# A three-layer block on one core: second evictions given to ScalarE and GpSimd, attention's weights prepared among the experts, more row buffers

## The chip, the cores and the metric

The kernel runs on one core of a Trainium2 chip. The metric is the device time of one execution in microseconds, lower is better. The core has TensorE (PE; its weight loads are listed as PEld), VectorE (DVE), ScalarE (ACT), GpSimd (POOL) and SyncE (SP), each with an instruction queue of its own that it works through in order, and DMA queues that move data between device memory and the on-chip memory SBUF. Matmul results land in PSUM.

## The reference: what is computed

```python
x = x + 0.5 * ffn(layernorm(x), router_w, rg, ru, rd, sg, su, sd)
x = x + attn(layernorm(x), w_qkv, ln_w, w_proj)
x = x + 0.5 * ffn(layernorm(x), router_w, rg, ru, rd, sg, su, sd)
```

`x` is (2, 2048, 256), that is 4096 tokens of width 256. `ffn` is a mixture of experts: a router takes the best two of 8 experts for each token, each expert takes at most 640 tokens in their order, computes `silu(x @ rg) * (x @ ru) @ rd` with inner width 1024, and its result is scaled by the routing weight and added to the token's row. A shared expert of inner width 2048 runs over all tokens and is added. `attn` works in groups of 64 tokens with 16 heads of width 16: one product for q, k and v, a root-mean-square norm of q and k with the weight `ln_w`, causal softmax inside the group, and an output product with `w_proj`.

## The kernel before, in words

Every float32 operand of a large product is split into two float16 parts (`split`, line 102 on ScalarE and 103 on VectorE), and three of the four partial products are summed in PSUM. The work runs in four phases.

- Phase a (0 to about 300 us): 32 row tiles of 128 tokens are loaded, normalised, routed, and their rows (tile `X`: 256 values and four tags) are scattered by GpSimd (line 283) to the experts' lists in device memory. Beside this, the shared expert runs over the first 4 of 8 blocks of 512 tokens.
- Phase b (to 614 us): the eight experts of the first feed-forward layer. Each runs 8 chunks of 128 inner columns. A chunk loads `re` and `re2` (lines 396 and 399), splits them into `wc` and `wd`, runs the gate and up products (`gate_up`, line 302), and one chunk later the down product (`down`, line 326). After the last chunk, five row tiles leave PSUM: VectorE or ScalarE writes a scaled row tile `eo` (lines 421 and 419), and GpSimd adds it to the rows of the accumulator `acc` by an indirect DMA (line 422). `eo` has 4 buffers.
- Phase c (to 1461 us): the shared expert over the last 4 blocks of the first layer and the first 7 of the second, 11 blocks in all. Between its chunks stand the steps of 32 attention tiles (`attn_tile`), each of which also normalises and routes its rows for the second layer and writes them to `X` (6 buffers). `attn_init` prepares attention's weights at the start: six pieces of float32 weights are loaded (`rq` line 442, `rp` line 448) and split.
- Phase d (to the end): the eight experts of the second layer, and the last block of the shared expert with `late=10`, which loads the residual rows in its tenth chunk.

A shared block has 16 chunks. In each, the first product `pgu` passes through ScalarE and VectorE (`sl`, lines 309, 310, 315; in phase a lines 313 and 315), ScalarE rounds it to `hh` (line 317) and VectorE takes the remainder `hl` (line 318). The down product of a chunk is emitted after the gate and up products of the following one (`defer`). After the last down product, both output tiles `outs[0]` and `outs[1]` are evicted: VectorE adds the scaled PSUM tile to the residual tile `xr` (line 359), and SP stores it (line 362).

The order of instructions on each engine comes from a planner that simulates the program while it is compiled: the written order gives the priority, and an instruction that the planner holds to be ready may go ahead of one that is not. The engines then follow that order. `drive` sets how the steps of attention tiles are woven into the chunks (one round of steps for every three chunk steps in phase c). A pool gives each named tile a number of buffers, and a new tile waits until the oldest buffer's users are done. Indirect adds to `acc` are put in a group of accesses that need not wait for one another.

Of the kernel before, what the change touches and what calls it, by code (L numbers as in the profile page):

```python
# [8 lines left out]
F32 = mybir.dt.float32  # L9
F32R = mybir.dt.float32r  # L10
F16 = mybir.dt.float16
# [4 lines left out]
ALU = mybir.AluOpType  # L16
# [4 lines left out]
P = 128  # L21
H = 256
# [3 lines left out]
WS = 16.0  # L26
XP = UP * WS
NB = 8
BT = 512
# [8 lines left out]
class Net:  # L38
# [306 lines left out]
    def shared(self, b, xb, src, dst, tanh=False, late=2):  # L345
        nc = self.nc
        outs = [self.ps_out.tile([P, BT], F32, name="po", tag="po") for _ in range(2)]
        for c in range(16):
            if c == late:
                res = self.res_load(src, b)  # L350
            h = [a[:, 0:BT] for a in self.hbuf()]
            yield from self.gate_up(self.sgu[:, c], xb, h, tanh)

            def fin(c=c, h=h):
                self.down(outs, 4, h, self.sdw[:, :, c], c, 16)
                if c < 15:
                    return
                for i in range(2):
                    nc.vector.scalar_tensor_tensor(
                        out=res[i], in0=outs[i].rearrange("p (t f) -> p t f", f=H), scalar=0.5 / WS,  # L360
                        in1=res[i], op0=ALU.mult, op1=ALU.add)
                    nc.sync.dma_start(
                        out=dst[b * BT + i * 2 * P:b * BT + (i + 1) * 2 * P].rearrange("(t p) f -> p t f", p=P),
                        in_=res[i])

            self.defer(fin)
            yield
# [14 lines left out]
            out=w, in0=tag[:, :, 3], scalar=float(e), in1=tag[:, :, 1], op0=ALU.is_equal, op1=ALU.mult)  # L382
        nc.vector.tensor_tensor(out=w, in0=w, in1=tag[:, :, 2], op=ALU.add)

    def experts(self, R, rg, ru, rd, cur):

        nc = self.nc
        for e in range(E):
            x, ids, wts = cur["x"], cur["id"], cur["w"]
            outs = [self.ps_out.tile([P, BT], F32, name="po", tag="po") for _ in range(3)]  # L390
            cur = {}
            nxt = self.expert_load(R, e + 1, cur) if e < E - 1 else iter(())
            for c in range(8):
                r = self.raw.tile([P, 2, 2, P], F32, name="re", tag="raw")
                for i, s in enumerate((rg, ru)):
                    nc.sync.dma_start(
                        out=r[:, i], in_=s[e, :, c * P:(c + 1) * P].rearrange("(k p) f -> p k f", p=P))
                r2 = self.raw.tile([P, H], F32, name="re2", tag="raw2")
                nc.sync.dma_start(out=r2, in_=rd[e, c * P:(c + 1) * P])
                wc = self.raw.tile([P, 2, 2, 2, P], F16, name="wc")  # L400
                self.split(wc[:, 0], wc[:, 1], r)
                wd = self.raw.tile([P, 2, H], F16, name="wd")
                self.split(wd[:, 0], wd[:, 1], r2)
                h = self.hbuf()
                for t0, n in SUBS:
                    hs = [a[:, t0:t0 + n] for a in h]
                    for _ in self.gate_up(wc, x[:, :, t0:t0 + n], hs):
                        pass

                def fin(e=e, c=c, h=h, wd=wd, outs=outs, ids=ids, wts=wts):  # L410
                    self.down(outs, 5, h, wd, c, 8)
                    if c < 7:
                        return
                    key = R["key"], e
                    for t in range(5):
                        eo = self.raw.tile([P, H], F32, name="eo", bufs=4)
                        o = outs[t // 2][:, (t % 2) * H:(t % 2 + 1) * H]
                        if t % 2:
                            nc.scalar.activation(eo, o, AF.Copy, scale=wts[:, t:t + 1])
                        else:  # L420
                            nc.vector.tensor_scalar_mul(eo, o, wts[:, t:t + 1])
                        i = nc.gpsimd.indirect_dma_start(  # L422
                            out=R["acc"][:, :], out_offset=bass.IndirectOffsetOnAxis(ap=ids[:, t:t + 1], axis=0),
                            in_=eo, in_offset=None, bounds_check=T - 1, oob_is_err=False, compute_op=ALU.add).ins
                        if t:
                            self.tc.declare_no_dep(i, group=str(key), reason="an expert's tokens are distinct")
                        self.tc.add_to_no_dep_group(str(key), i)

                self.defer(fin)
                next(nxt, None)  # L430
            for _ in nxt:
                pass

    def attn_init(self, w_qkv, ln_w, w_proj):
        nc = self.nc
        a = self.at
        self.wqkv = a.tile([P, 2, 2, 3 * H], F16, name="wqkv")
        self.wpr = a.tile([P, 2, 2, H], F16, name="wpr")
        for k in range(2):
            for c0, n in ((0, 2 * H), (2 * H, H)):  # L440
                r = a.tile([P, 2 * H], F32, name="rq", tag="q32")[:, :n]
                nc.sync.dma_start(out=r, in_=w_qkv[k * P:(k + 1) * P, c0:c0 + n])
                self.split(self.wqkv[:, 0, k, c0:c0 + n], self.wqkv[:, 1, k, c0:c0 + n], r)
        wp = w_proj.rearrange("(j r c) f -> r j c f", r=2, c=16)
        for k in range(2):
            r = a.tile([P, H], F32, name="rp", tag="yy")
            for j in range(8):
                nc.sync.dma_start(out=r[j * 16:(j + 1) * 16], in_=wp[k, j])
            self.split(self.wpr[:, 0, k], self.wpr[:, 1, k], r)
        self.lnw = a.tile([P, H], F32, name="lnw")  # L450
        nc.sync.dma_start(out=self.lnw, in_=ln_w.unsqueeze(0).to_broadcast([P, H]))
        self.mask = a.tile([P, 64], F32, name="mask")
        m2 = self.sm.tile([P, 64], F32, name="m2", bufs=1)
        for m, base in ((self.mask, 0), (m2, -64)):
            nc.gpsimd.memset(m, 0.0)
            nc.gpsimd.affine_select(
                out=m, in_=m, pattern=[[-1, 64]], compare_op=ALU.is_ge, fill=-3.0e38,
                base=base, channel_multiplier=1)
        nc.vector.tensor_copy(self.mask[64:P], m2[64:P])
        self.QK = a.tile([P, 24, P], F16, name="QK")  # L460
        nc.gpsimd.memset(self.QK, 0.0)
        self.V2 = []
        for i in range(2):
            v = a.tile([P, 2, 2, 8, 34], F16, name=f"V2{i}")
            nc.gpsimd.memset(v[:, :, 0, :, 32:33], 1.0)
            nc.gpsimd.memset(v[:, :, 1, :, 32:33], 0.0)
            self.V2.append(v)
# [199 lines left out]
def run_slots(tiles, until):  # L667
    while not until():
        for _ in tiles.steps():
            pass  # L670


def drive(main, tiles, rate):

    credit = 0.0
    side = iter(())
    for _ in main:
        credit += 1.0
        for _ in range(2):
            if next(side, "end") == "end":  # L680
                break
        if credit >= rate:
            for _ in side:
                pass
            credit -= rate
            if not tiles.done():
                side = tiles.steps()
    for _ in side:
        pass
# [3 lines left out]
def macaron(ctx, tc, x, w_qkv, ln_w, w_proj, router_w, rg, ru, rd, sg, su, sd, out):  # L693
    nc = tc.nc
    x = x.rearrange("b s h -> (b s) h")
    out = out.rearrange("b s h -> (b s) h")
    n = Net(ctx, tc)
    R1 = n.route_init(0)
# [32 lines left out]
    def ready(h, b):  # L731
        return lambda: (h, b) in fbs and fbs[(h, b)]["n"] == 4

    def all_shared(key, b, src, dst, **k):
        yield from n.shared(b, fbs[key]["xb"], src, dst, **k)
        used.add(key)
# [10 lines left out]
    with n.phase("a", BT, 2, 10):  # L747
# [16 lines left out]
        cur = {}  # L764
        for _ in n.expert_load(R1, 0, cur):
            pass
    with n.phase("b", CAP, 3):
        n.experts(R1, rg, ru, rd, cur)
    with n.phase("c", BT, 2, 6, SLC):
        n.attn_init(w_qkv, ln_w, w_proj)  # L770
        tiles = Tiles(tile2, 32, GAP_C)
        for b in range(NA, NB):
            drive(all_shared((1, b), b, R1["acc"], R1["acc"], tanh=True), tiles, RATE_C)
        for b in range(NC):
            run_slots(tiles, ready(2, b))
            drive(all_shared((2, b), b, x2, R2["acc"], tanh=True), tiles, RATE_C)
        run_slots(tiles, tiles.done)
        cur = {}
        for _ in n.expert_load(R2, 0, cur):
            pass  # L780
# [16 lines left out]
SLC = 2  # L797
# [28 lines left out]
```

## Time and profile before

| What | Value |
|---|---|
| Median of 3 runs | 1846.73 us (1844.07 to 1847.13) |
| The profiled execution's own time | 1844.18 us |
| Its span from first to last instruction | 1842.5 us |
| TensorE busy | 1782.8 us (97%) |
| VectorE busy | 1204.9 us (65%) |
| ScalarE busy | 952.2 us (52%) |
| GpSimd busy | 769.5 us (42%) |
| Granted TensorE clock | 0.999 |
| Scatters of rows (line 283) | 128, 1026 ns each on GpSimd |
| Adds to the accumulators (line 422) | 80, about 1610 ns each on GpSimd |

The page lists busy times of each engine, and groups of instructions by line. A row of the timeline gives start, duration, engine, line, operation, output and inputs, and in brackets the time the engine stood idle before it and what ended that wait. Matmuls overlap, so a busy TensorE in the page can still have short gaps between the starts of its matmuls.

### The profile page before, as it was taken

To read this page: it belongs to the slowest core of one execution; us is meant where nothing else is said; L and a number is where in the kernel's file an instruction comes from. 1 tells how busy PE (TensorE), PEld (TensorE's weight loads), DVE (VectorE), ACT (ScalarE), POOL (GpSimd) and SP (SyncE) were. 2 spreads that over 40 slices of the span, in tenths; PEclk is the share of its full clock that TensorE was granted. 3 is DMA by queue.
4 is the path that set the end of the run, shared out by engine and by line. 5 is a ranking of instruction groups with operands and counts; after the bars stand their busy time and mean duration, and the time that the engine had idled before them with its cause. 6 is when DMAs were issued, how large, how long until landed. Compare 5 with 4: busy or idle time off the path is not lost.

```text
span 1842.5 us, 37619 instructions
## 1 busy us (share of the span) xinstructions
PE 1782.8 (97%) x13722; PEld 1197.0 (65%) x13722; DVE 1204.9 (65%) x2869; ACT 952.2 (52%) x2055; POOL 769.5 (42%) x1104
## 2 busy tenths in 40 slices
PE   6989999999999899999999999999999999999999
PEld 3545656777777556666666666666665677777765
DVE  7665545666666567787877878787755565666643
ACT  5333324555555365766666666666333455555542
POOL 7776540111221244567667676776530011112210
PEclk9999999999999999999999999999999999999999
DMA  9753022445554246767585776757213044455420
GB/s 291 224 142 94 12 63 69 107 107 114 128 115 101 58 80 110 118 114 158 104 148 117 140 137 119 152 98 125 48 30 87 27 111 111 108 112 127 104 47 12
DMA packets 447514, 196.61 MB, mean 107 GB/s; under 512 B 302369, under 2 KB 444381, under 8 KB 447264
## 3 DMA queue, kind: packets, MB, share of 16 engines
q1 hardware_dynamic: 429664, 173.03, 42.7%
q0 software_dynamic: 17664, 21.17, 6.7%
q8 instruction: 107, 1.75, 0.4%
q14 instruction: 79, 0.65, 0.1%
HBM read 81.04 MB, written 52.85 MB: 73 GB/s over the span
## 4 chain that ended last, share of the span: by engine, by line
PE 57%; POOL 12%; issue 11%; DVE 10%; DMA 5%; ACT 4%; SPq 1%; POOLq 0%; DVEq 0%; another core or an unknown queue 0%; ACTq 0%
PE pgu L302 36%; PE po L326 18%; POOL xg L283 3%; DVE sl L315 2%; DVE sl L310 1%; POOL X L281 1%; DVE hl L318 1%; POOL rstd L142 1%; POOL S L546 1%; DMA y<-in_L_attn_x_dram 1%; ACT hh L317 1%; PE pqk L599 1%; ACT sl L309 1%; POOL e L557 1%; DMA xg<-X,di 1%
## 5 line engine op out<-in xcount | busy, mean ns | idle before, releaser
L302 PE MATMUL pgu<-xb,sgu 128*128 128x512 f16 x3072 | 743.5, 380 | 20.3 <-DVE sl L310 8.0
L317 ACT CAST hh<-sl 128x512 f16<-128x512 f32 (+2 forms) x512 | 272.9, 533 | 485.4 <-DVE sl L315 471.4
L302 PE MATMUL pgu<-xe,wc 128*128 128x384 f16 (+1 forms) x3072 | 497.0, 299 | 0.8
L302 PEld LDWEIGHTS <-sgu 128*128 128x128 f16 x3072 | 294.0, 98 | 295.7 <-issue 29.6
L315 DVE SCALAR_TENSOR_TENSOR sl<-pgu,sl 128x512 f32<-128x512 f32 (+2 forms) x512 | 300.6, 587 | 215.5 <-PE pgu L302 180.1
L318 DVE TENSOR_TENSOR hl<-sl,hh 128x512 f16<-128x512 f32 (+2 forms) x512 | 311.0, 608 | 160.1 <-ACT hh L317 153.3
L326 PEld LDWEIGHTS <-hh 128*128 128x128 f16 x3328 | 319.8, 98 | 114.9 <-ACT hh L317 13.9
L302 PEld LDWEIGHTS <-wc 128*128 128x128 f16 x3072 | 300.5, 98 | 94.1 <-issue 1.9
L326 PE MATMUL po<-sdw,hh 128*128 128x256 f16 x2048 | 349.9, 273 | 10.1 <-ACT hh L317 6.8
L326 PE MATMUL po<-sdw,hl 128*128 128x256 f16 x1024 | 247.5, 273 | 11.7 <-DVE hl L318 10.4
L326 PE MATMUL po<-wd,hh 128*128 128x256 f16 x1280 | 223.6, 273 | 0.0
L326 PEld LDWEIGHTS <-hl 128*128 128x128 f16 x1664 | 162.8, 98 | 57.2 <-DVE hl L318 23.3
L422 POOL DMA_INDIRECT out_dram<-eo,eid x40 | 64.1, 1604 | 314.3 <-DVE hl L318 244.9
L313 ACT ACTIVATE sl<-pgu 128x384 f32<-128x384 f32 (+1 forms) x336 | 158.9, 473 | 56.7 <-PE pgu L302 27.6
L422 POOL DMA_INDIRECT acc<-eo,eid x40 | 64.8, 1621 | 266.2 <-DVE hl L318 227.4
L283 POOL DMA_INDIRECT xg<-X,di x128 | 131.3, 1026 | 66.2 <-issue 27.5
L326 PE MATMUL po<-wd,hl 128*128 128x256 f16 x640 | 152.5, 273 | 2.1 <-DVE hl L318 1.9
L310 DVE SCALAR_TENSOR_TENSOR sl<-sl,pgu 128x512 f32<-128x512 f32 x176 | 120.0, 682 | 45.4 <-ACT sl L309 43.2
L309 ACT ACTIVATE sl<-pgu 128x512 f32<-128x512 f32 x176 | 104.3, 593 | 42.3 <-PE pgu L302 36.3
L102 ACT ACTIVATE wc<-re 128x512 f16<-128x512 f32 x128 | 80.5, 629 | 78.0 <-PE pgu L302 51.2
L103 DVE SCALAR_TENSOR_TENSOR wc<-re,wc 128x512 f16<-128x512 f32 x128 | 88.3, 690 | 25.9 <-ACT wc L102 25.7
L546 POOL TENSOR_TENSOR S<-S,amx 128x1024 f32<-128x1024 f32 x32 | 62.1, 1939 | 79.1 <-DVE amx L545 72.1
(141 smaller groups left out, 1740.6 us busy)
## 6 DMA issues: line engine op xcount, KB each, us to landing
re<-in_L_ffn_rg_dram SPq DMA_DIRECT2D x128, 128.0 KB
re<-in_L_ffn_ru_dram SPq DMA_DIRECT2D x128, 128.0 KB
re<-in_L_ffn_rd_dram SPq DMA_DIRECT2D x128, 128.0 KB
xg<-zero SPq DMA_DIRECT2D x16, 650.0 KB
y<-acc SPq DMA_DIRECT2D x64, 128.0 KB
y<-in_L_attn_x_dram SPq DMA_DIRECT2D x32, 128.0 KB
acc<-xr SPq DMA_DIRECT2D x16, 256.0 KB
out_dram<-xr SPq DMA_DIRECT2D x16, 256.0 KB
```

The lines of the kernel that those rows point to most:

```text
L103: nc.vector.scalar_tensor_tensor(out=lo, in0=src, scalar=WS, in1=hi, op0=ALU.mult, op1=ALU.subtract)
L283: i = nc.gpsimd.indirect_dma_start(out=R["xg"][:, :], out_offset=bass.IndirectOffsetOnAxis(ap=di[:, t, k:k + 1], axis=0), in_=X, in_offset ...
L302: nc.tensor.matmul(p, lhsT=wc[:, w, i, k, :], rhs=x[:, 2 * a + k, :], start=(j == 0), stop=(j == 5))
L309: nc.scalar.activation(s, p, AF.Tanh, scale=0.5 / XP)
L310: nc.vector.scalar_tensor_tensor(out=s, in0=s, scalar=1.0, in1=p, op0=ALU.add, op1=ALU.mult)
L313: nc.scalar.activation(s, p, AF.Silu, scale=1.0 / XP)
L315: nc.vector.scalar_tensor_tensor(out=s, in0=ps[1], scalar=1.0 / XP / (2.0 * XP if tanh else 1.0), in1=s, op0=ALU.mult, op1=ALU.mult)
L317: nc.scalar.copy(h[0], s)
L318: nc.vector.tensor_tensor(out=h[1], in0=s, in1=h[0], op=ALU.subtract)
L326: nc.tensor.matmul(o, lhsT=h[a][:, t * P:(t + 1) * P], rhs=wd[:, w], start=(c == 0 and j == 0 and t % 2 == 0), stop=(c == nch - 1 and j == 2),
L422: i = nc.gpsimd.indirect_dma_start(out=R["acc"][:, :], out_offset=bass.IndirectOffsetOnAxis(ap=ids[:, t:t + 1], axis=0), in_=eo, in_offset ...
L546: self.anchor = nc.gpsimd.tensor_tensor(out=S, in0=S, in1=mx.unsqueeze(2).to_broadcast([P, 16, 64]), op=ALU.subtract)
```

## The change

Four edits. The second of the two evictions of a shared block is done by ScalarE, which scales the PSUM tile into a new SBUF tile `ev`, and GpSimd, which adds it to the residual tile; the last block of the kernel (`late=10`) keeps VectorE for both. The loads and splits of attention's weights move from `attn_init` into a generator `attn_weights`, of which `experts` takes one step in the sixth chunk of each expert of phase b, six steps in all; the raw pieces use the buffers of the experts' raw weights (`raw` and `raw2`, two each), and the split weights stay in the pool that lives for the whole kernel. `eo` gets 5 buffers instead of 4, and the fifth indirect add of an expert is no longer exempt from waiting for the four before it. `X` gets 10 buffers in phase c instead of 6.

```diff
                 for i in range(2):
-                    nc.vector.scalar_tensor_tensor(
-                        out=res[i], in0=outs[i].rearrange("p (t f) -> p t f", f=H), scalar=0.5 / WS,
-                        in1=res[i], op0=ALU.mult, op1=ALU.add)
+                    o = outs[i].rearrange("p (t f) -> p t f", f=H)
+                    if i == 0 or late > 2:
+                        nc.vector.scalar_tensor_tensor(
+                            out=res[i], in0=o, scalar=0.5 / WS, in1=res[i], op0=ALU.mult, op1=ALU.add)
+                    else:
+                        ev = self.tok.tile([P, 2, H], F32, name="ev", bufs=1)
+                        nc.scalar.mul(ev, o, 0.5 / WS)
+                        nc.gpsimd.tensor_tensor(out=res[i], in0=ev, in1=res[i], op=ALU.add)
                     nc.sync.dma_start(
...
-    def experts(self, R, rg, ru, rd, cur):
+    def experts(self, R, rg, ru, rd, cur, also=iter(())):
...
-                        eo = self.raw.tile([P, H], F32, name="eo", bufs=4)
+                        eo = self.raw.tile([P, H], F32, name="eo", bufs=5)
...
-                        if t:
+                        if 0 < t < 4:
                             self.tc.declare_no_dep(i, group=str(key), reason="an expert's tokens are distinct")
                         self.tc.add_to_no_dep_group(str(key), i)
 
                 self.defer(fin)
                 next(nxt, None)
+                if c == 5:
+                    next(also, None)
...
-    def attn_init(self, w_qkv, ln_w, w_proj):
-        nc = self.nc
-        a = self.at
-        self.wqkv = a.tile([P, 2, 2, 3 * H], F16, name="wqkv")
-        self.wpr = a.tile([P, 2, 2, H], F16, name="wpr")
+    def attn_weights(self, w_qkv, w_proj):
+
+        nc = self.nc
+        self.wqkv = self.cst.tile([P, 2, 2, 3 * H], F16, name="wqkv")
+        self.wpr = self.cst.tile([P, 2, 2, H], F16, name="wpr")
         for k in range(2):
             for c0, n in ((0, 2 * H), (2 * H, H)):
-                r = a.tile([P, 2 * H], F32, name="rq", tag="q32")[:, :n]
+                r = self.raw.tile([P, 2 * H], F32, name="rq", tag="raw")[:, :n]
                 nc.sync.dma_start(out=r, in_=w_qkv[k * P:(k + 1) * P, c0:c0 + n])
                 self.split(self.wqkv[:, 0, k, c0:c0 + n], self.wqkv[:, 1, k, c0:c0 + n], r)
+                yield
         wp = w_proj.rearrange("(j r c) f -> r j c f", r=2, c=16)
         for k in range(2):
-            r = a.tile([P, H], F32, name="rp", tag="yy")
+            r = self.raw.tile([P, H], F32, name="rp", tag="raw2")
             for j in range(8):
                 nc.sync.dma_start(out=r[j * 16:(j + 1) * 16], in_=wp[k, j])
             self.split(self.wpr[:, 0, k], self.wpr[:, 1, k], r)
+            yield
+
+    def attn_init(self, ln_w):
+        nc = self.nc
+        a = self.at
...
-        n.experts(R1, rg, ru, rd, cur)
-    with n.phase("c", BT, 2, 6, SLC):
-        n.attn_init(w_qkv, ln_w, w_proj)
+        n.experts(R1, rg, ru, rd, cur, n.attn_weights(w_qkv, w_proj))
+    with n.phase("c", BT, 2, 10, SLC):
+        n.attn_init(ln_w)
```

## The prediction

> **What bounds the kernel now.** I read the page's engine totals, then busy time by stage. The stages start at 300 (first experts), 614 (attention beside shared blocks), 1345 (attention done), 1461 (second experts) and 1781 us (last shared block).
>
> ```profile
> PE 1782.8 (97%) x13722; PEld 1197.0 (65%) x13722; DVE 1204.9 (65%) x2869; ACT 952.2 (52%) x2055; POOL 769.5 (42%) x1104
> ...
> 0.00:300.00 300.00, 268.51 (x1774) 157.50 (x1775) 174.79 (x540) 107.25 (x228) 172.47 (x363) 0.99 0.47 131
> 300.00:614.00 314.00, 312.89 (x2486) 242.78 (x2485) 191.08 (x413) 166.36 (x393) 58.73 (x41) 1.00 0.47 105
> 614.00:650.00 36.00, 30.14 (x173) 16.19 (x171) 20.39 (x46) 12.42 (x25) 13.75 (x16) 1.00 0.41 92
> 650.00:1345.00 695.00, 682.54 (x5715) 431.70 (x5714) 538.34 (x1309) 442.67 (x921) 445.18 (x608) 1.00 0.64 118
> ```
>
> Columns: window, length, then PE, PEld, DVE, ACT, POOL busy. TensorE is the bound everywhere; only its idle time can be won. Since recorded matmuls overlap, I take gaps from matmul starts: back to back, 512 columns are 0.216 us apart and 256 columns 0.109. Summing what exceeds that gives 36.4 us idle before 300, 2.1 in the first experts, 7.2 in 614 to 650, 15.3 in 650 to 1345, 3.0 to 1461, 2.6 in the second experts. Next, who makes the gaps: the waits of 300 to 614, 1461 to 1842 and 614 to 650.
>
> ```profile
> DVE eo L421 <- DMA acc<-eo,eid: 13.4, 7, 2.6
> ...
> DVE eo L421 <- DMA out_dram<-eo,eid: 17.9, 8, 3.8
> ...
> ACT wqkv L102 <- DMA rq<-in_L_attn_w_qkv_dram: 10.3, 4, 4.0
> ```
>
> The fifth scaled row waits for the first scatter to free one of four buffers (total us, times, longest); ScalarE waits for attention's raw weights. The timeline shows what TensorE pays, at 347, 623 and 637, then at a block boundary of the attention stage.
>
> ```profile
> 346.89 0.48 DVE L421 TENSOR_SCALAR eo<-po,ew 128x256 f32<-128x256 f32 x1 [2.60 <-DMA acc<-eo,eid]
> 347.76 0.28 PE L326 MATMUL po<-wd,hl 128*128 128x256 f16 x1 [0.54 <-DVE hl L318]
> ...
> 622.55 0.48 DVE L421 TENSOR_SCALAR eo<-po,ew 128x256 f32<-128x256 f32 x1 [2.33 <-DMA acc<-eo,eid]
> 623.69 2.75 PE L302 MATMUL pgu<-xb,sgu 128*128 128x512 f16 x12 [1.96 <-DVE sl L315]
> ...
> 637.81 0.61 PE L326 MATMUL po<-sdw,hh 128*128 128x256 f16 x4 [1.16 <-ACT hh L317]
> ...
> 1018.73 0.68 DVE L540 TENSOR_TENSOR S<-psc,mask 128x512 f32<-128x512 f32 x1
> 1019.32 0.68 DVE L359 SCALAR_TENSOR_TENSOR xr<-po,xr 128x512 f32<-128x512 f32 x1
> 1019.92 0.68 DVE L318 TENSOR_TENSOR hl<-sl,hh 128x512 f16<-128x512 f32 x1
> 1020.66 0.28 PE L326 MATMUL po<-sdw,hl 128*128 128x256 f16 x1 [0.71 <-DVE hl L318]
> ```
>
> A block's second eviction stands on VectorE just ahead of the hl that TensorE waits for.
>
> [...] the accumulating scatter here frees its row after 3.9 us (618.65 to 622.55), so I use 3.9.
>
> **The change part by part**, against the profiled execution, 1844.18 us (span 1842.5 and 1.7 around it).
>
> Five scaled rows: the 15 waits above vanish, and so should the gaps behind them: 0.71+0.30, 0.24+0.30 and 0.25+0.30 in the first experts, 0.69+0.30, 1.03+0.30 and 0.30 in the second: 4.7 us. The other waits (mostly 1.6 us) cost TensorE nothing. I take -4.3 (bounds -3.0 and -4.7). The stall goes to GpSimd: t=4 is no longer exempt, so its scatter waits until t=0 to 3 have landed. Queued behind it are the next experts' id casts, not needed for some 30 us. At the end of the first experts scatter 3 starts at 624.21, lands at 628.1, and scatter 4 lands at 632.0 instead of 629.97. In the last block, scatters land some 4 us later than 1790 and the residual load (issued at 1790) is used at 1838: 44 us of cover; without it, 4 us.
>
> Start of the attention stage: gaps of 0.55+2.12 come from the fifth row; 0.57, 1.33, 0.86, 0.22, 1.02, 0.50 (4.5) fall while ScalarE and VectorE take the weights between shared chunks. The first attention load, now behind 4 rq and 16 rp issues on SP (635.51), can go at 632.0. GpSimd's constant fills shift behind scatter 4, to about 634; first used at 655.8. What is late next is the first rows' load and VectorE's statistics behind it (1.4 us waited for y now). I take 2.5 of the 2.7 and 2.7 of the 4.5: -5.2 (bounds -2.7 and -7.2).
>
> Weights among the first experts: ScalarE gets 2x0.629+2x0.416+2x0.414 = 2.9 us, VectorE 2x0.693+2x0.411+2x0.554 = 3.3, SP 4x0.346+16x0.414 = 8.0, in a 314 us stage where they are busy 166 and 191 us and SP issues three loads per 4.9 us chunk. Each piece takes one of two raw buffers, so the next chunk's load starts a chunk later; it took two chunks ahead, so one is left. The danger is ScalarE standing in order before a piece that has not landed: at 633 to 642 it waited 4.0, 2.45 and 3.64. From the fifth-row waits TensorE forgives some 1.6 (2.13 cost 0.54). So 0 to 6x2.4 = 14; I take +1.2, because these loads go out a chunk ahead.
>
> Evictions, 15 of 16 blocks: VectorE loses 0.68 per block; ScalarE gains an estimated 0.60 (128x512 f32 from PSUM, L309: 593 ns), GpSimd 1.18 (128x512 QK subtract, L524). At six boundaries (858 to 1262) hl costs TensorE 0.87; without L359 hl can start 0.6 sooner: 6x0.6 = 3.6. ScalarE idles 1.04 us there before hh (1018.25), GpSimd 3.3 before S (1021.88), so both fit. The second store, and SP behind it, waits for GpSimd instead of VectorE: about 1019.3 against 1020.0. But VectorE's gap may be filled by the 1.21 us maximum (L545) instead, and ScalarE's slot may be missed. I take -2.6 (bounds -6 and, as below, +20).
>
> In the first stage the same edit adds 4x1.18 to GpSimd (busy 172 of 300), among scatters whose landing ScalarE's X waits for (42.6 us there), and takes 2.7 from VectorE: between -2.7 and +4.7, I take +1.0.
>
> Ten X rows: in 650 to 1345 no X write waits for a scatter, so 0; the transfers are already covered by a tile interval of some 20 us. Uncovered, it would be the first stage's wait, up to 6.2 us each.
>
> Sum: -4.3-5.2+1.2-2.6+1.0 = -9.9, so 1834.3 profiled. The median of the runs stands 1.00138 above the profiled execution (1846.73/1844.18): **1836.8**.
>
> **Rivals.** (A) As summed, chance 0.58, 1831 to 1842. (B) More: with VectorE lighter and attention started earlier, the 1.04 us gaps ahead of each boundary (L310 late behind ScalarE) close too, 10 of the 15.3 us instead of 2.6: 1844.18-17.3 = 1826.9, 1829.4 as median. For it: both gaps recur every 80.7 us. Against: the first comes from ScalarE, which gets more work. 0.15. (C) A wait takes the place of the one removed: each of the six weight pieces holds ScalarE 3.1 us, 1.5 beyond what is forgiven, +9 for +1.2: -2.1, median 1844.6, within noise. For it: the 10.3 us now. Against: one chunk of lead. 0.14. (D) Slower: ScalarE's eviction, in order, lands ahead of the gate's L309 and hh at each boundary of the attention stage (+0.60), and VectorE's gap takes L545 (+1.21): 1.8 us for 11 blocks, +20 in place of -2.6: 1856.9, median 1859. It decides from (7.3+3.7)/11 = 1.0 us per block. For it: ScalarE already makes L309 late at 1016.11. Against: the idle 1.04 us. 0.13.
>
> **How the numbers follow.** 0.2% (3.7 us) is about what a measurement here can tell from no change. A and B are faster, 0.73; C is no change, 0.14; D slower, 0.13. 1829 to 1849 holds A, most of B and C, and the near end of D.
>
> **What would show it.** Right: no eo wait ended by a scatter's landing on VectorE, such waits on GpSimd's fifth scatter instead; no wqkv wait after 614 and under 3 us idle in 614 to 650; hl gaps at boundaries under 0.4; first y load near 632. Wrong: ScalarE waits for rq or rp among the experts with gaps behind them; gaps above 1.9 us per boundary; GpSimd's add ending the waits of SP's transposes; more than 40 us idle before 300.

## The result and the profile after

The changed kernel takes 1852.99 us (median of 6 runs, 1850.99 to 1856.16), beside 1846.25 us for the kernel before on the same chip. The ratio is 1.0037, with a 95% interval of 1.0023 to 1.0050: a little slower, where the prediction had 1836.8. The profiled executions stand at 1844.18 us before and 1856.16 us after (spans 1842.5 and 1854.4), so the two traces have 12 us between them. That is more than the 6.7 us between the medians, since the profiled execution of the changed kernel is the slowest of its six. A few lines have moved in the new code: the fifth-row eviction is now line 426 (VectorE) and 424 (ScalarE), the indirect add 427, the id cast 385, the tag load 380, the raw attention weights `rq` 449 and `rp` 456, the first eviction of a block 361, and the new pair 365 and 366.

The engine totals of the changed kernel, then the stages that the prediction showed, with the same columns (window, length, PE, PEld, DVE, ACT, POOL busy, PEclk, DMA share, GB/s). The windows follow the stages; that of the first experts is longer by 13 us:

```profile
PE 1788.9 (96%) x13722; PEld 1200.8 (65%) x13722; DVE 1203.8 (65%) x2854; ACT 961.9 (52%) x2070; POOL 793.5 (43%) x1119
```

```profile
300.00:627.00 327.00, 317.83 (x2492) 245.35 (x2491) 195.12 (x419) 169.96 (x401) 57.06 (x42) 0.98 0.46 104
627.00:663.00 36.00, 31.32 (x174) 17.60 (x172) 18.52 (x45) 12.53 (x24) 16.75 (x20) 0.91 0.38 81
663.00:1345.00 682.00, 672.77 (x5649) 425.75 (x5647) 526.34 (x1277) 439.67 (x915) 454.09 (x602) 1.00 0.60 117
```

Same matmuls, same count, but TensorE is 9.2 us short of its stage among the first experts (1.1 before), and the granted clock, 1.00 in both stages before, is 0.98 there and 0.91 at the start of attention. Two things are mixed in that: TensorE waits, and after some waits its matmuls run slower.

The table gives, for each stage, its length and the time by which the starts of matmuls exceed back-to-back spacing (idle and slow together), worked out in the manner of the prediction (its figures for the kernel before are up to 1.8 us lower). Starts are taken because the records overlap: in the kernel before a matmul of 512 columns in line 302 is recorded with 380 ns on average, and back to back the starts lie 216 ns apart. First experts means from the first to the last gate and up matmul of the phase.

| Stage | before: length, lost | after: length, lost | lost, change |
|---|---|---|---|
| up to the first experts | 297.5, 38.2 | 298.6, 39.2 | +1.0 |
| first experts | 316.2, 2.2 | 328.6, 14.7 | +12.5 |
| next 36 us (attention starts) | 36, 7.3 | 36, 8.1 | +0.8 |
| rest, to the second experts | 806.4, 19.1 | 803.6, 15.6 | -3.5 |
| second experts | 316.9, 2.9 | 318.4, 4.4 | +1.5 |
| last block, to the last matmul | 65.3, 0.6 | 65.3, 0.6 | 0 |

**The first experts hold nearly the whole loss;** what the other stages gain and lose comes to about nothing. The fifth-row waits on VectorE are gone, as predicted. The waits of 302 to 627 us name what came instead (us in total, times, longest):

```profile
ACT wqkv L102 <- DMA rq<-in_L_attn_w_qkv_dram: 20.4, 4, 6.3
...
POOL acc L427 <- DMA acc<-eo,eid: 7.0, 2, 3.6
```

ScalarE stands before the split of attention's raw weights for 20.4 us, twice the 10.3 us that it stood there at the start of attention before. The waits of SP's own queue in the same window tell why the weights are late:

```profile
SPq L380 <- POOL eid L385: 27.3, 4, 7.4
```

SP stands before the load of an expert's tags, because the tag's buffer is held by GpSimd's id cast. This wait is not new. In the kernel before it is nearly as long:

```profile
SPq L375 <- POOL eid L380: 26.7, 4, 7.1
```

What is new is that a load of raw weights now stands behind three of these four tag loads, and that the first of them goes out 4.3 us later, counted from the start of the experts. The timeline around 360 us puts the links in order (start, duration, engine, line; in brackets the idle time before it and what ended it):

```profile
355.08 1.55 POOL L427 DMA_INDIRECT acc<-eo,eid  x1 [3.54 <-DVE sl L315]
359.14 0.19 POOL L385 CAST eid<-tag 128x5 int32<-128x5 f32 x1 [2.51 <-DMA acc<-eo,eid]
359.36 0.37 SPq L380 DMA_DIRECT2D tag<-xg  x1
359.84 0.46 SPq L449 DMA_DIRECT2D rq<-in_L_attn_w_qkv_dram  x1
362.50 0.42 ACT L102 ACTIVATE wqkv<-rq 128x256 f16<-128x256 f32 x1 [6.14 <-DMA rq<-in_L_attn_w_qkv_dram]
363.37 1.03 PE L326 MATMUL po<-wd,hh 128*128 128x256 f16 x4 [2.70 <-ACT hh L317]
364.20 2.12 PE L302 MATMUL pgu<-xe,wc 128*128 128x384 f16 x6
...
368.67 1.14 PE L302 MATMUL pgu<-xe,wc 128*128 128x384 f16 x6
```

Read it from the top. The fifth indirect add, no longer exempt, stands 3.54 us until its predecessors have landed and starts at 355.08. (The bracket names VectorE's `sl`; but in e1 below, where this add is exempt, it starts 0.30 us after its predecessor's end.) Its landing frees the id buffer that the next expert's cast at 359.14 needs; in the kernel before, whose experts begin 1.0 us earlier, that cast stood at 353.83. The cast frees `tag`; SP issues the tag load, and behind it, in order, the `rq` load. ScalarE reaches the split of `rq` 6.14 us before the data, and the `hh` that TensorE needs is queued behind it. TensorE loses 2.87 us at 360.34, 3.19 at 403.76 and 2.54 at 447.82, in three of the eight experts. The first of the four pieces, at 319 us, was waited for 2.15 us and cost nothing.

The last two lines of the fence show a second loss. The same six matmuls of 384 columns take 2.12 us just after the gap and 1.14 us four microseconds later: their starts lie at double spacing. This lasts some 3 us after each of the three gaps and loses 1.4, 1.7 and 1.7 us; the last section shows when it happens. A fourth gap, of 1.23 us at 303.67, belongs to the evictions (below).

**At the start of attention** the weight gaps have gone, but a wait of VectorE has grown from 1.4 to 7.5 us. Timeline of the changed kernel:

```profile
642.00 1.55 POOL L427 DMA_INDIRECT acc<-eo,eid  x1 [2.89 <-issue]
645.80 0.33 SPq L487 DMA_DIRECT2D y<-acc  x1
647.86 0.43 DVE L137 BATCH_NORM_STATS2 st<-y 128x6 f32<-128x256 f32 x1 [7.51 <-DMA y<-acc]
648.92 2.19 PE L302 MATMUL pgu<-xb,sgu 128*128 128x512 f16 x6 [3.45 <-DVE sl L310]
```

The first row load follows the landing of the fifth indirect add, and VectorE stands in order before the statistics of those rows while the shared block's `sl` waits behind them. TensorE loses 3.61 and 1.27 us, and 2.6 more at double spacing.

**Inside the attention stage** the evictions do what was forecast. One block boundary, from the timeline:

```profile
1030.90 0.68 DVE L361 SCALAR_TENSOR_TENSOR xr<-po,xr 128x512 f32<-128x512 f32 x1
1031.02 0.62 ACT L317 CAST hh<-sl 128x512 f16<-128x512 f32 x1 [1.04 <-DVE sl L315]
...
1031.50 0.68 DVE L553 TENSOR_TENSOR S<-psc,mask 128x512 f32<-128x512 f32 x1
...
1031.55 0.59 ACT L365 ACTIVATE ev<-po 128x512 f32<-128x512 f32 x1
1032.04 0.59 ACT L309 ACTIVATE sl<-pgu 128x512 f32<-128x512 f32 x1
1032.10 0.68 DVE L318 TENSOR_TENSOR hl<-sl,hh 128x512 f16<-128x512 f32 x1
1032.22 1.69 POOL L366 TENSOR_TENSOR xr<-ev,xr 128x512 f32<-128x512 f32 x1 [0.86 <-ACT ev L365]
...
1032.35 0.38 PE L326 MATMUL po<-sdw,hh 128*128 128x256 f16 x2
...
1032.84 0.28 PE L326 MATMUL po<-sdw,hl 128*128 128x256 f16 x1
```

Only one eviction (line 361) stands on VectorE now, ScalarE takes the other in a place where `hh` is already out, GpSimd adds it with nobody waiting, and the gap before `hl` is 0.27 us instead of 0.87. The 1.04 us gap ahead of the boundary stays.

**At the end of a phase** the same edit loses. Timeline where the attention stage gives way to the second experts:

```profile
1472.14 0.60 ACT L365 ACTIVATE ev<-po 128x512 f32<-128x512 f32 x1 [3.94 <-PE po L326]
1472.75 1.28 ACT L313 ACT_TABLE_LOAD   x1
```

There is no tile work left to put ahead, so ScalarE stands 3.94 us before the eviction, and behind it stand a table load of 1.28 us and the first Silu of the experts. TensorE loses 2.71 us at 1471.77, 1.7 more at double spacing, and 1.23 at 303.67 where the first experts begin.

### The profile page after: what moved, and what is told of

It reads as the page before. It is cut to its first block, busy times and chain, and to the rows that moved or that the text cites. A ratio compares the mean times of both kernels' runs of the same rounds, so it can differ in the third digit from the quotient of the medians.

```text
span 1854.4 us, 37595 instructions
## 1 busy us (share of the span) xinstructions
PE 1788.9 (96%) x13722; PEld 1200.8 (65%) x13722; DVE 1203.8 (65%) x2854; ACT 961.9 (52%) x2070; POOL 793.5 (43%) x1119
## 4 chain that ended last, share of the span: by engine, by line
PE 59%; POOL 10%; DVE 9%; issue 9%; DMA 6%; ACT 4%; SPq 1%; another core or an unknown queue 0%; POOLq 0%; DVEq 0%; ACTq 0%
PE pgu L302 38%; PE po L326 19%; POOL xg L283 3%; DVE sl L315 2%; DVE sl L310 1%; DMA xg<-X,di 1%; DVE hl L318 1%; POOL X L281 1%; DMA xg<-zero 1%; POOL rstd L142 1%; DMA acc<-eo,eid 1%; PE pqk L612 1%; ACT hh L317 1%; ACT sl L309 1%; POOL e L570 1%
## 5 line engine op out<-in xcount | busy, mean ns | idle before, releaser
L302 PE MATMUL pgu<-xe,wc 128*128 128x384 f16 (+1 forms) x3072 | 502.7, 301 | 3.6 <-ACT sl L313 3.6
L326 PE MATMUL po<-sdw,hh 128*128 128x256 f16 x2048 | 350.3, 273 | 11.3 <-ACT hh L317 7.2
L563 ACT COPY V<-vs 64x512 f16<-64x512 f16 x128 | 78.8, 616 | 28.3 <-PE py L581 24.9
```

The source lines that it names most:

```text
L302: nc.tensor.matmul(p, lhsT=wc[:, w, i, k, :], rhs=x[:, 2 * a + k, :], start=(j == 0), stop=(j == 5))
L326: nc.tensor.matmul(o, lhsT=h[a][:, t * P:(t + 1) * P], rhs=wd[:, w], start=(c == 0 and j == 0 and t % 2 == 0), stop=(c == nch - 1 and j == 2),
```

## The experiments

Each kernel is timed against the kernel before on the same chip; ratios are to it, with the 95% interval. "Lost" is TensorE's idle and slow time as in the table above.

### e1: after, with the fifth indirect add exempt again

```diff
-                        if 0 < t < 4:
+                        if 0 < t < (4 if e == E - 1 else 5):
```

(The last expert's fifth add keeps its wait; exempting that one too was not tried.)

> The changed kernel, with the fifth add exempt from waiting again, except in the last expert of each layer. Theory 1 (the fifth add's wait holds back the id cast, the tag load behind it on SP, and so attention's raw weights behind that): the raw loads go out about 3 us earlier, the three gaps of 2.5 to 3.2 us in the first experts fall under 1 us each, their half-speed stretches go, the stage from first to last expert matmul is within 4 us of the 316.2 us before (328.6 in the changed kernel), and the run is at 1843 to 1846. The gap at the start of attention (3.6 us) stays, since the last expert still waits. Theory 2 (ScalarE's order alone puts the split too early; the fifth add has no part in it): three gaps of over 2 us stay, stage at 326 or more, run at 1851 to 1854.

Measured: 1844.10 us, 1.0006 (0.9997 to 1.0015). The first experts lose 6.1 us instead of 14.7; three gaps of 1.41, 1.99 and 1.42 remain, above the 1 us expected, and none is followed by slow matmuls. So the wait of the fifth add is the larger part of the loss, and not all of it.

### e2: before, with the weights among the experts alone

```diff
-        n.experts(R1, rg, ru, rd, cur)
+        n.experts(R1, rg, ru, rd, cur, n.attn_weights(w_qkv, w_proj))
...
-        n.attn_init(w_qkv, ln_w, w_proj)
+        n.attn_init(ln_w)
```

> The kernel before with attention's weights prepared among the experts and nothing else. Theory 1: without the fifth add's wait the raw loads go out earlier, stage of the first experts at most 3 us longer than 316.2, idle in the first 36 us of attention 3 to 5 us instead of 7.2: 1842 to 1847. Theory 2: stage 10 us or more longer, run at 1852 to 1857.

Measured: 1847.98 us, 1.0027 (1.0016 to 1.0039). The first experts lose 6.1 us (2.2 before): three gaps of 0.98, 1.95 and 1.64, where ScalarE waits for `rq` 16.2 us in four waits, at most 5.0. So the weights hold ScalarE even without the fifth add's wait: 3.9 us against the +1.2 taken. The start of attention loses 5.7 us, from 7.3. But the kernels whose code is as before at that place (before, e4, e6, e10) range from 4.3 to 7.3 there, so an improvement is not shown. All three figures expected are missed, by up to 1 us.

### e3: before, with five scaled rows and the fifth add's wait alone

```diff
-                        eo = self.raw.tile([P, H], F32, name="eo", bufs=4)
+                        eo = self.raw.tile([P, H], F32, name="eo", bufs=5)
...
-                        if t:
+                        if 0 < t < 4:
```

> The kernel before with five scaled-row buffers and the fifth add waiting, and nothing else. Theory 1: the wait as such costs TensorE nothing, since no attention weights stand behind it on SP; the fifth-row gaps (2.1 us in the first experts, 2.6 in the second) go; at the start of attention the first row load comes later. 1840 to 1846. Rival (the wait costs TensorE by itself, through the ids of the next expert): gaps at the starts of experts, 1849 or more.

Measured: 1844.50 us, 1.0010 (1.0001 to 1.0018). Both expert stages lose nothing now: 314.0 us each, 5.1 us better than before. The fifth add waits here as in the changed kernel, and the id casts are late too (the one that answers to 359.14 comes 60.0 us after the experts begin, 56.3 before and 60.6 in the changed kernel), but no weight load stands behind SP's tag load, and TensorE pays nothing. The gain is given back at the start of attention, where the raw weights now come later still: ScalarE waits up to 7.6 us for `rq`, with gaps of 4.29 and 2.24 us and about 4 us of double spacing behind them, and the rest of that stage loses 26.2 instead of 19.1 us. This trace is of an execution of 1847.31 us, 2.8 above the median, so it shows more of this loss than most executions have.

Together, e2 and e3 show that neither part alone makes the 12.5 us (11.3 without the 1.23 us gap of the evictions): the wait alone costs the experts nothing, the weights alone cost 3.9.

### e4: before, with the second eviction on ScalarE and GpSimd alone

The edit is the first part of the change's diff and nothing else.

> The kernel before with the second eviction on ScalarE and GpSimd in 15 of 16 blocks, and nothing else. Theory: hl gaps at six boundaries fall from 0.87 to 0.27 (-3.6); where a shared block is followed by experts ScalarE stands in order before the eviction with the experts' first Silu and its table load behind it, about 2.7 us plus 1.6 at half speed at the second layer and 1.2 at the first; +1 in the first stage: +2 to +4 in all, 1848 to 1851. Rival (as predicted, no cost at the ends of the phases): 1842 to 1844.

Measured: 1841.88 us, 0.9993 (0.9984 to 1.0002). A miss: a loss was expected, and there is none. The rest of the attention stage loses 15.1 instead of 19.1 us; the gaps at the phase ends came as expected, 1.23 us where the first experts begin and 2.72 at the end of the attention stage, but no slow matmuls behind the second. So the interior gains what was forecast or more, and the phase ends take it back.

### e5: after, with a third id buffer

```diff
-        ids = hold["id"] = self.sm.tile([P, 5], I32, name="eid")
+        ids = hold["id"] = self.sm.tile([P, 5], I32, name="eid", bufs=3)
```

This is the sharpest test of the chain: the fifth add still waits, the weights are still there, only an id cast now takes a buffer last used three experts ago, where it was two.

> The changed kernel, the fifth add waiting as it does there, but with three buffers for the experts' ids instead of two. Theory 1 says that the fifth add's wait reaches attention's weights only through the id cast (its buffer is free when the fifth add of two experts ago has landed) and the tag load behind it on SP: with a third buffer both no longer wait, the raw loads go out at least 3 us earlier, the first experts' stage is at most 320 us (328.6 in the changed kernel), and the run is at 1842 to 1846. If the wait reaches the weights by another way, the stage stays over 325 and the run over 1850. The 3.6 us gap at the start of attention stays in both.

Measured: 1837.17 us, 0.9975 (0.9964 to 0.9985), 11 us less than after by the ratios. The first experts lose 1.2 us. In this kernel's trace the fifth add stands 3.63 us, as in the changed kernel, and starts at 354.67, but SP and ScalarE do not follow it. Its timeline:

```profile
354.67 1.55 POOL L427 DMA_INDIRECT acc<-eo,eid  x1 [3.63 <-DVE sl L315]
355.42 0.34 SPq L449 DMA_DIRECT2D rq<-in_L_attn_w_qkv_dram  x1
...
357.51 0.42 ACT L102 ACTIVATE wqkv<-rq 128x256 f16<-128x256 f32 x1 [1.64 <-DMA rq<-in_L_attn_w_qkv_dram]
```

The load goes out 4.4 us earlier than in the changed kernel (359.84; 3.9 us earlier counted from the start of the experts), and ScalarE waits 1.64 instead of 6.14 us. Over the stage its wait for `rq` is 7.9 us in place of 20.4, which TensorE forgives: the stage's one remaining gap is the 1.23 us of the evictions. The id casts still wait for adds to land (9.2 us in three waits), but they run one expert further ahead: the tag load that needs the cast of 359.19 goes out only at 386.68, and SP no longer waits for an id cast in this stage. One buffer of 20 bytes per partition undoes the loss, and more than expected.

### e6: e4, with VectorE keeping the second eviction at the two phase ends

```diff
-                    if i == 0 or late > 2:
+                    if i == 0 or late > 2 or own:
...
-            drive(all_shared((2, b), b, x2, R2["acc"], tanh=True), tiles, RATE_C)
+            drive(all_shared((2, b), b, x2, R2["acc"], tanh=True, own=b == NC - 1), tiles, RATE_C)
```

(and `own=b == NA - 1` in phase a)

> The kernel before with the second eviction on ScalarE and GpSimd, except in the two blocks that experts follow (the fourth of phase a, the last of phase c), which stay with VectorE. Theory: the gaps of 1.23 and 2.72 us behind these two evictions go, the six boundaries keep 0.27: 3 to 5 us below the run with 15 evictions moved, 1837 to 1839. Rival (the two gaps have another cause, the experts' first Silu with its table load): no difference from that run, 1841 to 1843.

Measured: 1835.69 us, 0.9971 (0.9961 to 0.9981), 4 us below e4 by the ratios. The gaps at both phase ends are gone. So the evictions alone are worth 5 us where they stand between tiles.

### e7: after, with the edits of e1, e5 and e6

> The changed kernel with the three mends together: fifth add exempt but in the last expert of a layer, three id buffers, VectorE for the evictions that experts follow. From the parts: 1844.1 less about 4 for the two evictions, less up to 4.8 for the gaps of 1.4 to 2.0 among the experts: 1836 to 1841. If the waits merely move, 1843 or more.

Measured: 1831.16 us, 0.9945 (0.9928 to 0.9961), faster than the kernel before and the changed one, and below the 1836 to 1841 expected. Its busy time by stage, first experts and start of attention:

```profile
294.00:608.00 314.00, 314.00 (x2501) 244.60 (x2500) 196.68 (x422) 170.97 (x401) 55.37 (x40) 1.00 0.48 109
608.00:644.00 36.00, 30.96 (x174) 17.52 (x172) 18.63 (x45) 12.52 (x24) 16.73 (x20) 0.91 0.38 81
```

TensorE is busy in all of the 314.0 us of the experts, with the weights prepared inside. The start of attention is as in the changed kernel: VectorE stands 7.67 us before the first rows, and the first gap is 3.78 us. The next three kernels tried to remove that.

### e8: e7, with the first attention tile's statistics three steps later

```diff
-        yield
-        yield
+        for _ in range(5 if j == 0 else 2):
+            yield
```

> As the run before it, and the first attention tile takes three steps more between its row load and its statistics. The gap of over 3 us at the start of attention is VectorE standing in order before these statistics, whose rows come late behind the last expert's fifth add. If so the gap falls under 1.5 us and the run is 1 to 4 us faster than the one before it; if the gap comes from something else, no difference.

Measured: 1832.95 us, 0.9954 (0.9937 to 0.9971). A miss: VectorE still stands 7.43 us before the first statistics, the gap is 3.54 us.

### e9: e7, with all attention tiles begun two slots later

```diff
         tiles = Tiles(tile2, 32, GAP_C)
+        tiles.slot = -2
```

> The kernel with all mends (e7), with attention's tile steps begun two slots of shared work later (a slot is some 5 us, a quarter of the tile interval). What is removed is the order on VectorE at the start of the attention stage: the first rows' statistics standing 7.7 us ahead of the shared block's own instructions. Theory (VectorE stands in order before a row load that can only follow the landing of the last scatters): the 7.7 us wait and the 3.8 and 1.5 us gaps at 628 and after go, with the slow matmuls behind them, 3 to 6 us less than e7, 1825 to 1828 us. Rival (TensorE waits there for something else, such as the shared block's own start): the gap stays. Second rival (the attention chain of 32 tiles is what ends the stage, so 10 us of later start come back at the end of it): same as e7 or up to 10 us slower.

Measured: 1849.27 us, 1.0025 (1.0015 to 1.0034), 15 us slower than e7 by the ratios. VectorE's wait for the rows is down to 0.4 us, and another has its place. The timeline:

```profile
625.44 1.55 POOL L427 DMA_INDIRECT acc<-eo,eid  x1 [2.86 <-DVE sl L310]
...
629.21 2.66 POOL L474 MEMSET QK<- 128x3072 f16 x1 [2.06 <-DMA acc<-eo,eid]
...
631.92 0.24 POOL L469 TENSOR_SCALAR_AFFINE_SELECT mask<-mask 128x64 f32<-128x64 f32 x1
...
632.19 0.20 DVE L472 COPY mask<-m 64x64 f32<-64x64 f32 x1 [7.04 <-POOL mask L469]
...
632.82 0.43 DVE L137 BATCH_NORM_STATS2 st<-y 128x6 f32<-128x256 f32 x1 [0.43 <-DMA y<-acc]
```

VectorE now stands before the copy of the mask, which GpSimd finishes only behind the fill of `QK`, which waits for the last adds to land. The gap grew to 5.06 us. Moving the tiles also moved them against the blocks: from 850 us on each boundary loses 1.1, 0.47 and 0.85 us, where e7 loses 1.04 and 0.27. The six boundaries make about 7 of the 15 us; the rest lies in smaller gaps at both ends of the attention stage.

### e10: before, with ten X rows alone

```diff
-    with n.phase("c", BT, 2, 6, SLC):
+    with n.phase("c", BT, 2, 10, SLC):
```

> The kernel before with ten instead of six X row buffers in the attention stage, nothing else. My step: 0, because no X write waits for a scatter between 650 and 1345. Ratio 0.999 to 1.001. Rival: the buffers free scatters or their order and are part of the change's loss or gain, 2 us or more either way.

Measured: 1842.59 us, 0.9992 (0.9985 to 0.9999). Within 0.2% of no change, as costed.

### e11: after with e5 and e6, and idle copies on ScalarE in every expert

```diff
                 h = self.hbuf()
+                if c == 3:
+                    junk = self.raw.tile([P, P], F32, name="junk", bufs=1)
+                    for _ in range(5 + e + (4 if R is self.second else 0)):
+                        nc.scalar.copy(junk, r[:, 0, 0])
```

> The kernel after with three id buffers and VectorE's two evictions at the stage ends (e5 and e6 together), and in the fourth chunk of every expert 5 to 16 idle copies of 128x128 on ScalarE ahead of the Silu (5 to 12 in the first experts, 9 to 16 in the second), so that sixteen stalls of growing length reach TensorE; the copies' results are used by nothing. [...]

Measured: 1835.15 us, one run. The stalls did not come about: the planner spread the copies between ScalarE's other work (in the last expert, for instance, 4, 3, 1 and 2 at a time), and the expert stages lose 0.9 and 0.7 us. So the run says nothing of how the slow stretches of matmuls go with the length of the gap ahead of them, for which it was made; the last section takes that question from the traces. What this run, a single one, does show: ScalarE's busy time, first experts,

```profile
295.00:610.00 315.00, 314.40 (x2503) 244.71 (x2501) 195.77 (x421) 183.97 (x463) 58.22 (x40) 1.00 0.47 108
```

is 13 us above e7's 171, more than four times the 2.9 us of splits that the prediction counted, and TensorE pays less than 1 us. More work on ScalarE is hidden among the experts here; what TensorE pays for is ScalarE standing still before data that is late (6.14 us of it cost 2.87 in the changed kernel).

### e12: e7, with the tiles four slots later and the mask built among the experts

```diff
+        tiles.slot = -4
...
-        self.mask = a.tile([P, 64], F32, name="mask")
+        self.mask = self.cst.tile([P, 64], F32, name="mask")
```

(the mask's five instructions move from `attn_init` to the end of `attn_weights`)

> The kernel with all mends (e7), with attention's tile steps begun four slots later (a whole tile interval, some 20 us, so that tiles and blocks keep their alignment) and with the mask built among the first experts, so that at the start of the attention stage neither a row load nor GpSimd's fill of QK stands before VectorE's shared-block work. Theory (VectorE's in-order waits behind the last scatters are what TensorE waits for at the start, and the boundary gaps of e9 came from the shifted alignment): no gap above 1 us at the start, boundary gaps as in e7, 4 to 7 us less than e7: 1824 to 1828 us. Rival 1 (the chain of 32 tiles sets the end of the stage, or the alignment is not what doubled the boundary gaps): the gaps at the end or at the boundaries grow, 1831 us or more. Rival 2 (another consumer waits for the last scatters at the start): a gap of 3 us or more stays there.

Measured: 1849.39 us, 1.0028 (1.0018 to 1.0037). Another miss. VectorE's timeline again:

```profile
635.16 0.84 DVE L137 BATCH_NORM_STATS2 st<-y 128x6 f32<-128x256 f32 x2 [8.25 <-DMA y<-acc]
```

The statistics of the first rows stand before the shared block's work even with the tiles written four slots later, and the gap is 4.88 us. The boundaries lose some 2.5 us each, so the alignment that e9 was blamed on is not restored by a whole tile interval. Where the planner places the first statistics, and why the boundaries got worse in e9 and e12, stays open; so does whether the start of attention can be mended at all while the first row load must follow the landing of the last adds.

## Why the prediction was wrong, step by step

**Five scaled rows, -4.3: the gain was there, the price of its wait was not.** In e3 the expert stages gain 5.1 us. The step that failed is the sentence on the stall: "Queued behind it are the next experts' id casts, not needed for some 30 us." The ids themselves are not needed for that long. But the cast is the last reader of `tag`, SP's next tag load waits for it (27.3 us in four waits; 26.7 already in the kernel before), and what stands behind the tag load on SP was never asked. In the kernel before nothing urgent stood there; the change itself put the `rq` load there. Each part was costed alone, and the loss is in their meeting: e3 -2.2, e2 +3.9, both +12.5, of which 1.2 is the evictions' gap and 4.8 slow matmuls. The id cast needed a further look of the same kind on its other side, at what it waits for: a buffer that the late fifth add holds, as e5 shows.

**Weights among the experts, +1.2: right for a load that goes out a chunk ahead, and the reason given for that failed.** With three id buffers (e5) the `rq` loads no longer stand behind a waiting tag load, and the weights cost nothing: the 1.2 us still lost in the first experts is the evictions' gap, and in e7, with e6's edit, it is gone too. In e2, where only the weights move, they lost 3.9 us more than before, the mechanism of rival C at less than half its size. In the changed kernel ScalarE stood 5.8 to 6.3 us before three of the four pieces, and about 3.2 of each such wait was forgiven (6.14 cost 2.87, 6.25 cost 3.19), not the 1.6 taken from the fifth-row waits.

**Start of attention, -5.2: measured +0.8**, in a window that moves by 3 us between kernels with the same code there. The named gaps went, and the first row load goes out 18.7 us after the last expert product, where the prediction had 18.2. The prediction said what is late next, "the first rows' load and VectorE's statistics behind it", and counted nothing for it: VectorE's wait grew from 1.4 to 7.5 us, because the weight splits that used to fill it were gone and the fifth add lands later: it is 4.0 us with the weights alone moved (e2), 2.1 with the fifth add's wait alone (e3). The error is the cover: the work moved away was what hid this wait.

**Evictions, -2.6: measured -3.5 in the interior of the changed kernel and -4.0 in e4**, with six `hl` gaps down by 0.6 each as worked out (0.87 to 0.27 or 0.28, one to 0.63). ScalarE's eviction was estimated at 0.60 and took 0.59 or 0.60 us; GpSimd's add was estimated at 1.18 and takes 1.26 to 1.70. Rival D's mechanism, ScalarE's in-order eviction ahead of urgent work, did not show at the boundaries for which it was priced, and did at the two phase ends, which the sum did not contain: 2.71 + 1.7 and 1.23 us. In the changed kernel's trace the ends take about 2 us more than the interior gains.

**First stage, +1.0: measured +1.0**, though this stage moves by 2.7 us between kernels with the same code there (295.9 us in e1, 298.6 in the changed kernel), so that says little. **X rows, 0: right** (e10).

**A term that was missing: slow matmuls after a gap.** In the changed kernel about 9 us (1.4, 1.7, 1.7, 2.6, 1.7) of the time lost is matmuls at double spacing behind gaps in five places; after 126 us the kernel before has no such stretch. That is three quarters of the 12 us between the traces. The sum priced a gap at its length. In part this term is chance: the mean granted clock is 0.994 in the profiled execution and 0.995 to 0.997 in the five others, from which I estimate six stretches of 3.41 us at half clock in the one and three to five in the others.

Of the rivals none ended as described. The kernel was slower by 0.37%, with neither D's place nor its price. With the id buffer, the exemption and the phase ends mended, the ratio is 0.9945, where the prediction worked out 0.9946 (1834.3/1844.18): this is partly chance, since the start of attention is still not what the sum had, and e7 has mends that the sum did not.

## What to carry to other kernels

When a wait is moved to another engine, follow it through every queue: what the delayed instruction frees, which queue waits for that buffer, and what stands behind the waiter there, including what the same change has just put there. Cost edits together where they share a queue, not only one by one. A tiny tile (here ids of 128x5) with two buffers can be the link that carries a stall from one engine to three others, and a third buffer was the cheapest mend here (e5, 11 us less than the changed kernel).

## What the runs showed of the hardware

Some gaps in TensorE's work cost more than their length in these traces: behind them matmuls start at double spacing (six of 384 columns take 2.12 us at 364.20 in the changed kernel and 1.14 at 368.67), in four of its five places for 3.41 us and in one for 6.83. The length of the gap alone does not decide it. Gaps of 2.87, 3.19, 2.54 and 2.71 us (after), 2.40 (before), 4.29 and 2.24 (e3) did it, 1.94 in e3 did, and in e12 1.40 did, just behind another of 2.18; 2.31 us at 277 in the kernel before did not, nor did 2.39 in e10, nor the 2.71 of e4, which is the very gap that did it in the changed kernel. The granted clock on record tells the cases apart. Neighbouring windows at two gaps of the changed kernel (the third number from the end is the granted clock):

```profile
359.36:362.77 3.41, 1.31 (x10) 0.64 (x7) 0.00 (x0) 0.27 (x1) 0.00 (x0) 1.00 0.38 80
362.77:366.19 3.42, 2.82 (x11) 1.53 (x12) 2.56 (x6) 2.33 (x7) 0.00 (x0) 0.50 0.30 88
1472.11:1475.52 3.41, 0.93 (x8) 0.78 (x8) 0.80 (x3) 3.00 (x5) 1.26 (x1) 1.00 0.37 132
1475.52:1478.93 3.41, 3.41 (x13) 1.59 (x11) 1.81 (x4) 1.47 (x4) 0.00 (x0) 0.50 0.25 78
```

and at the gap of e4:

```profile
1455.83:1459.24 3.41, 1.73 (x16) 1.40 (x15) 0.69 (x1) 1.57 (x2) 0.91 (x1) 1.00 0.14 49
1459.24:1462.66 3.42, 2.56 (x18) 1.75 (x18) 2.11 (x5) 2.91 (x7) 0.35 (x1) 1.00 0.30 105
```

In the changed kernel the clock is at 0.50 from 362.77, 407.15, 451.52, 649.49 and 1475.52 us, each time for 3.41 us (6.83 the fourth time). These starts lie 13, 13, 58 and 242 times 3.413 us apart, while the first three gaps, at 360.34, 403.76 and 447.82, lie 12.7 and 12.9 times 3.413 us apart: the slow stretches keep to steps of 3.41 us, and the gaps do not. So I divided each trace into windows of 3.41 us in line with its own slow stretches, and took how long TensorE is idle inside each (3.41 us less the back-to-back time of the matmuls that start in it). Over the fourteen traces, from 25 to 1800 us and outside stretches already at half clock, all 29 windows with 2.14 us or more of idle time are followed by one at a clock of 0.50, none of the 7203 with less than 2.05 is, and 2 of the 12 between are. The gap of 2.71 us left 2.49 us in one window in the changed kernel; in e4 a border of two windows cut it into 1.87 and 0.88.

In the changed kernel a single window at half clock lost 1.4 to 1.7 us. By an estimate from these figures (2.05, 2.14, 3.41 and 1.7 us), a gap under 2.05 us costs this kernel its length, unless others share its window, and one of 2.1 to 4.3 us may cost up to 1.7 us more, depending on where it falls. No run here varied the gap alone; this rests on gaps that came about by themselves.
